# The first image's statistics ahead of the weights, and two input places in the second pass, in a two-layer convolution kernel

## The chip, the cores and the metric

The kernel runs on one core of a Trainium2 chip. The metric is the device time of one execution in microseconds (us). The engines are PE (TensorE), DVE (VectorE), ACT (ScalarE), POOL (GpSimd) and SP (SyncE), whose queue issues all of the kernel's transfers.

## The reference

The input x is 4 images of 64 channels and 256 x 256 pixels, in float32. Two layers follow each other, each with a residual.

```python
x = x + L0(_gn(x), ...)      # group norm, 32 groups
x = x + L1(_gn(x), ...)

# layer 0
h = gelu(conv3x3(x, c1_w) + c1_b)
xa, k = split(c1x1(h, c2_w, c2_b))                 # 64 channels each
xs = gelu(depthwise 3x1 (depthwise 1x3 (xa)))
mask = top 2 of 3 of softmax(mean(xs) @ gate_w.T)
out = xs + sum over 3 experts of mask * w3(w2(k) * w1(xs))     # ranks 2, 4, 8
return c1x1(out, proj_w, proj_b)

# layer 1
h = relu(batchnorm(conv3x3(x, quantized w1) + b1))
h = batchnorm(conv3x3(h, quantized w2) + b2)
return relu(h + x)
```

Quantizing needs the greatest absolute value of all weights of w1 and of w2: `round(w / scale)` with `scale = max|w| / 127`. The batch norms take their mean and variance over all four images, so each is a point at which everything before must be done.

## The kernel before

**Data.** An image lies in memory as 128 partitions (64 channels twice, for two rows) by 128 row pairs. A chunk is 8 row pairs (1 MB), 16 chunks an image, 64 in all. x, the result of layer 0 (t1), the input of layer 1 (y), and the two convolution results of layer 1 (h1, h2) go through DRAM in chunks.

**Head.** `weights()` (from L201) comes first. It loads three packed arrays, `mset` (960 KB: w1, w2, and two factors), `m64` (129 KB) and `m128` (612 KB), and makes from them everything that later steps need: `av`, `sh_bias`, `tap_bias`, `ends`, `outer`; by four small matmuls (L238, L247, L250, L253), which share one PSUM place, `wk`, `k_bias`, `pw3` and `pb3`; and the quantized `wq` for w1 and w2. For the last, DVE takes the maximum of each partition (L263), POOL takes the maximum over the partitions with `partition_all_reduce` (L265), and DVE scales, rounds and copies (L267 to L278). After that the 16 chunks of image 0 are loaded and DVE takes their statistics (L403); the first two working chunks of x are loaded (L481); POOL makes the first row sums and differences `front_v` (L501); `stats_end` turns the statistics into the normalized convolution weights `c1s` and `u12` and its bias.

**Loop.** Everything then goes by a written plan: `at(step, order, call, ...)` puts a call into a step at a place in it, and the plan is run in the order of its keys with each engine's instructions kept in that order. A step is 8 rows of one image in layer 0 (`F_STEPS` = 32 steps an image). In it PE runs the products of the first convolution (`front_conv_a`, `front_conv_b`), the taps (`front_taps_a`, `front_taps_b`) and the projection (all by `quarter`, L458); DVE does `front_butterfly` (L568, L569), the taps' horizontal part and the next image's statistics; POOL does `front_pad` (L488), `front_v` (L501) and `divide` (L451), a one-column memset called `tick`, which waits for PE and for which PE's next products wait. Layer 1's first pass (`conv1_*`) follows image by image.

**Second pass.** With `ss1` known, `conv2_load` (L1089) brings chunk i+3 of h1, ACT normalizes it (`conv2_affine`, L1094), ACT and DVE split it into two parts (`conv2_split`, L360 and L362), POOL adds neighbouring pixels (`conv2_add`, L367), and PE convolves (L316). The result goes to h2, except for the last `KEEP` chunks, which stay on chip.

**Places.** Inputs lie in a pool `ring` of three places and a pool `spare` of one. Layer 0 and layer 1's first pass take the spare place in every fifth or fourth chunk; the second pass loads into the ring alone and keeps one h2 chunk in the spare place.

**End.** For each chunk, with the kept ones first, y is loaded (L1203), ACT makes v = y * gn + shift (L1215), DVE makes h = h * ss2 + v (L1216) and max(h, 0) + y (L1217), and SP writes the output (L1219) and reads an h2 chunk (L1224) into a place that came free.

Of the kernel before, what the change touches and what calls it, by code (L numbers as in the profile page):

```python
# [9 lines left out]
F32 = mybir.dt.float32  # L10
# [44 lines left out]
NLOW = sum(LOWS)  # L55
GN_EPS = 1e-5
BN_EPS = 1e-5
KEEP = 14
QMAX = 127.0
ROUND = 12582912.0  # L60

# [2 lines left out]
def conv_preact_kernel(ctx: ExitStack, tc: tile.TileContext, io, col128, colset, col64):  # L64
# [4 lines left out]

    const = ctx.enter_context(tc.tile_pool(name="const", bufs=1))  # L70
    stat = ctx.enter_context(tc.tile_pool(name="stat", bufs=2))
    ring = ctx.enter_context(tc.tile_pool(name="ring", bufs=3))
    spare = ctx.enter_context(tc.tile_pool(name="spare", bufs=1))
    psum = ctx.enter_context(tc.tile_pool(name="psum", bufs=1, space=PSUM))
    dram = ctx.enter_context(tc.tile_pool(name="dram", bufs=1, space=DRAM))
# [20 lines left out]
    def flat(t):  # L96
        return t.rearrange("p a b -> p (a b)")

    RING = max(CPAIR * PW, (CPAIR + 1) * W)

    def place_in(name, fourth=False):
        return (spare if fourth else ring).tile([P, RING], F32, tag="in", name=name)

    def chunk_in(name, fourth):

        t = place_in(name, fourth)
        return t[:, 0 : CPAIR * PW].rearrange("p (a b) -> p a b", b=PW)

    def dense_in(name, n, fourth=False):

        return place_in(name, fourth)[:, 0 : n * W].rearrange("p (a b) -> p a b", b=W)

    layers = ExitStack()

# [58 lines left out]
    nc.vector.memset(eps, GN_EPS)  # L173
    eps_bn = const.tile([P, 1], F32, name="eps_bn")
    nc.vector.memset(eps_bn, BN_EPS)
    ones = const.tile([P, P], F32, name="ones")
    nc.vector.memset(ones, 1.0)
    zeros = const.tile([P, PW], F32, name="zeros")
    nc.vector.memset(zeros, 0.0)
# [18 lines left out]
    w_scale = {n: column(f"scale_{n}") for n in ("w1", "w2")}  # L198
    sh = c128("sh")

    def weights():  # L201

        mset = flat(chunk_x("mset"))[:, 0 : io["mset"].shape[1]]
        m64_t = work.tile([P, 2, GF], F32, tag="xs", name="m64", bufs=4)
        m64 = flat(m64_t)[0:C, 0 : io["m64"].shape[1]]
        nc.sync.dma_start(mset, io["mset"])
        nc.sync.dma_start(m64, io["m64"])
        nc.sync.dma_start(m128, io["m128"])

# [14 lines left out]
        nc.vector.tensor_scalar(tap_bias, sv_sum, sh_bias, c128("sv_b"), ALU.mult, ALU.add)  # L224
        for i in range(2):
            nc.vector.tensor_scalar(end[:, i : i + 1], sh[:, 2 * i : 2 * i + 1], c128("c2_ba"), None, ALU.mult)
        nc.vector.tensor_scalar(ends, end, sv_sum, None, ALU.mult)
        for i in range(2):
            o = outer[:, i, :]
            nc.vector.tensor_scalar(o, zeros[:, 0:W], sh_bias, None, ALU.add)  # L230
            nc.vector.tensor_tensor(o[:, 0 : W : W - 1], o[:, 0 : W : W - 1], end, ALU.subtract)
            nc.vector.tensor_scalar(o, o, c128("sv")[:, 2 * i : 2 * i + 1], None, ALU.mult)

        nc.vector.memset(wk, 0.0)
        ps = small("ps_wk")
        nc.tensor.matmul(ps[:, 0:NLOW], c64("c2_k"), c64("w2_t")[:, 0:NLOW], start=True, stop=True)  # L238

        for s in range(2):  # L240
            half = slice(s * C, s * C + C)
            for i in range(2):
                o = 16 * (i ^ s)
                nc.vector.tensor_copy(wk[half, s, i, o : o + NLOW], ps[half, 0:NLOW])
        nc.vector.memset(both, 0.0)
        ps = small("ps_kb")
        nc.tensor.matmul(ps[:, 0:1], c64("w2_t"), c64("c2_bk"), start=True, stop=True)  # L247
        nc.vector.tensor_tensor(k_bias, ps[:, 0:1], c128("e_b2"), ALU.add)
        ps = small("ps_pw3")
        nc.tensor.matmul(ps[:, 0:C], c64("w3"), c64("proj_t")[:, 0:C], start=True, stop=True)  # L250
        nc.vector.tensor_copy(pw3, ps[:, 0:C])
        ps = small("ps_pb3")
        nc.tensor.matmul(ps[:, 0:3], c64("proj_t"), c64("b3"), start=True, stop=True)  # L253
        nc.vector.tensor_copy(pb3, ps[:, 0:3])

        for name in ("w1", "w2"):  # L260
            w = cset(name)
            top = stat.tile([P, 1], F32, tag="s1", name=f"top_{name}")
            nc.vector.tensor_reduce(top, w, AX.X, ALU.max, apply_absolute_value=True)  # L263
            top_all = stat.tile([P, 1], F32, tag="s2", name=f"top_all_{name}")
            nc.gpsimd.partition_all_reduce(top_all, top, P, bass_isa.ReduceOp.max)  # L265
            scale = w_scale[name]
            nc.vector.tensor_scalar(scale, top_all, 1.0 / QMAX, None, ALU.mult)  # L267
# [201 lines left out]
    def front_alloc(b, k):  # L469
        c = b * NCH + k  # L470
        if c % 5 == 3:
            xs_of[b, k] = chunk_x(f"x_{b}_{k}")
        else:
            xs_of[b, k] = chunk_in(f"x_{b}_{k}", c % 5 == 4)

    def front_load(b, k):

# [328 lines left out]
    y_in, h_out, st_h = {}, {}, {}  # L806

    def conv1_load(b, k):
        y = y_in[b, k] = dense_in(f"yn_{b}_{k}", CPAIR + 1, k % 4 == 0)
        a = 1 if k == 0 else 0  # L810
        at_y = y[:, a:, :]
        nc.sync.dma_start(at_y, y_d[b][:, k * CPAIR + a - 1 : (k + 1) * CPAIR, :])
# [76 lines left out]
        nc.vector.bn_aggr(bn1[:, b, :], flat(st_h.pop(b)))  # L889


    weights()
    STATS_IN = (("s", 4),) * 4 + (("o", 3),) * 3
    for k in range(NCH):
        stats_load(0, k, *STATS_IN[k % 7])
# [2 lines left out]
    for k in range(2):  # L898
        front_alloc(0, k)
        front_load(0, k)  # L900

    first_v = ((0, 0), (0, 1), (1, 0))
    for n, half in first_v:
# [8 lines left out]
    for n, half in first_v:  # L912
        front_v(0, n, half, ((0, 3),))

    def at_each(places, chain):

        for place in places:
            at(*place, next, chain, None)

    F_STEPS = NOCT  # L920
    CONV1 = B * F_STEPS
# [185 lines left out]
        del h_in[i]  # L1107
        split_sums(sums2[i % 2], sums_in.pop(i))

    for i in range(3):  # L1110
        conv2_load(i)
    ss1 = const.tile([P, 2], F32, name="ss1")
    bn_affine(bn1, "g1", "be1", ss1, "bn1")
# [9 lines left out]

    def chunk_h2(b, k):
        n = next(h2_place) % KEEP
        if n == KEEP - 1:
            h2[b, k] = dense_in(f"h2_{b}_{k}", CPAIR, True)
        else:
            h2[b, k] = kept.tile([P, CPAIR, W], F32, tag="h2", name=f"h2_{b}_{k}", bufs=KEEP - 1)
        return h2[b, k]  # L1130

    def conv2(d):
# [23 lines left out]
    with tc.manual_schedule(  # L1156
        engines={
            mybir.EngineType.PE,
            mybir.EngineType.SP,
            mybir.EngineType.DVE,  # L1160
            mybir.EngineType.Pool,
            mybir.EngineType.Activation,
        }
    ):
        for cut in CUTS:
            conv2_affine(0, *cut)
            conv2_split(0, (cut,))
        conv2_add(0)
        conv2_sums(0)
        conv2_affine(1)  # L1170
        conv2_add(1)
        for d in range(2 * len(chunks)):
            i = d // 2
            opened = conv2(d)
            if d % 2 == 0:
                if i + 3 < len(chunks):
                    conv2_load(i + 3)
                if i + 1 < len(chunks):
                    conv2_split(i + 1)
                    conv2_sums(i + 1)  # L1180
            elif i + 2 < len(chunks):
                conv2_affine(i + 2)
                conv2_add(i + 2)
            conv2_out(d, *opened)


# [4 lines left out]

    halves_stack.close()
    end = ctx.enter_context(tc.tile_pool(name="end", bufs=2, reuse_waits="tile"))
    MORE = 6
    AHEAD = 3 + MORE - 1

    def end_load(i):
        b, k = steps[i]
        if i % (3 + MORE) < 3:
# [10 lines left out]
    for i, (b, k) in enumerate(steps):  # L1210
        if i + AHEAD < len(steps):
            end_load(i + AHEAD)
        y, h = y_of.pop(i), h2.pop((b, k))
        v = end.tile([P, CPAIR, W], F32, tag="v", name=f"v_{b}_{k}")
        nc.scalar.activation(v, y, AF.Identity, bias=shift[:, b : b + 1], scale=gn2[b][:, 1:2])  # L1215
        nc.vector.scalar_tensor_tensor(h, h, ss2[:, 0:1], v, ALU.mult, ALU.add)  # L1216
        nc.vector.scalar_tensor_tensor(h, h, 0.0, y, ALU.max, ALU.add)  # L1217
        for par in range(2):
            nc.sync.dma_start(out_v[b, par][:, k * CPAIR : (k + 1) * CPAIR, :], h[par * C : (par + 1) * C])  # L1219
# [117 lines left out]
```

## Time and profile before

| | |
|---|---|
| time, median of 3 runs | 3260.03 us (3255.96 to 3262.79) |
| time of the profiled execution | 3257.65 us |
| its span, first to last instruction | 3255.8 us |
| PE busy | 2664.0 us (82%) |
| DVE busy | 2665.1 us (82%) |
| ACT busy | 1647.6 us (51%) |
| POOL busy | 1603.1 us (49%) |
| moved by DMA | 832.01 MB, 256 GB/s in the mean |
| mean granted clock of TensorE | 0.924 |

How to read it: a row of a time line gives the start in us, the busy time in us, the engine, the line, the operation, what it writes and reads, how many instructions are merged in it, and in brackets the engine's idle time before it with what ended that. "SPq" and "POOLq" are queues: issuing and configuring, not counted as busy. "PEld" is TensorE's weight load. A digit of a slice row is the busy share of a fortieth of the span (81.4 us) in tenths.

### The profile page before, as it was taken

How to read it: one execution, taken by the hardware profiler on the slowest of the kernel's cores; microseconds unless marked ns; L12 is line 12 of the kernel's file. 1: busy time of each engine (PE TensorE's matmuls, PEld its weight loads, DVE VectorE, ACT ScalarE, POOL GpSimd, SP SyncE). 2: the span in 40 equal slices, each digit the busy share in tenths (PEclk: the TensorE clock that was granted, in tenths of full speed). 3: DMA queues.
4: the chain of work that ended last, by engine and by line, in shares of the span. 5: the costliest groups of instructions: out<-in, count | busy, mean ns of one | idle time of the engine just before them, and what ended most of it. 6: DMA issues, size and time to landing. Idle time of an engine off the chain costs nothing.

```text
span 3255.8 us, 61027 instructions
## 1 busy us (share of the span) xinstructions
PE 2664.0 (82%) x25080; PEld 1756.5 (54%) x25080; DVE 2665.1 (82%) x2810; ACT 1647.6 (51%) x1799; POOL 1603.1 (49%) x1833
## 2 busy tenths in 40 slices
PE   2999999999999999999999999989999999300000
PEld 1555555555555555555676677768787878200000
DVE  7676588878888777777899999979999999876655
ACT  0444443444434344446666666767777777432222
POOL 2444544444444534445687787757777777100000
PEclk9999999999999999999999999999999999655555
DMA  8665689879987777766788886656666663799999
GB/s 306 175 182 131 161 270 287 246 212 289 277 272 219 217 203 210 214 195 207 283 288 298 292 315 220 245 194 229 238 234 233 245 223 124 261 412 412 413 412 377
DMA packets 355591, 832.01 MB, mean 256 GB/s; under 512 B 22192, under 2 KB 284848, under 8 KB 293360
## 3 DMA queue, kind: packets, MB, share of 16 engines
q1 hardware_dynamic: 355312, 828.11, 76.5%
q8 instruction: 197, 3.23, 0.4%
q14 instruction: 82, 0.67, 0.1%
HBM read 489.85 MB, written 338.17 MB: 254 GB/s over the span
## 4 chain that ended last, share of the span: by engine, by line
PE 40%; SPq 10%; DVE 8%; DMA 3%; issue 3%; ACT 2%; POOL 1%; ACTq 0%; DVEq 0%; POOLq 0%
PE ps_h L316 22%; SPq L1224 7%; PE ps_c L458 5%; PE ps_h2m L316 4%; PE ps_a L458 3%; SPq L1219 2%; PE ps_hm L316 2%; DVE half L362 2%; DMA yn<-y_d 2%; DVE h L342 2%; PE ps_o L778 1%; PE ps_p L458 1%; SPq L1203 1%; DVE st_h L874 1%; DMA y_end<-y_d 1%
## 5 line engine op out<-in xcount | busy, mean ns | idle before, releaser
L316 PE MATMUL ps_h<-half,w_q 128*128 128x512 f32 x4096 | 1026.4, 402 | 20.4 <-DVE h L342 13.7
L316 PEld LDWEIGHTS ps_h<-half,w_q 128*128 128x128 f32 x4096 | 772.7, 190 | 249.4 <-DVE h L342 24.0
L381 POOL TENSOR_TENSOR sum<-s,sum 128x640 fp32r<-128x640 f32 (+1 forms) x256 | 557.2, 2197 | 199.4 <-ACT sum L379 193.8
L501 POOL TENSOR_TENSOR v_ring<-x 128x256 f32<-128x256 f32 x1024 | 591.2, 613 | 48.4 <-DMA x<-in_x 46.5
L458 PE MATMUL ps_c<-v_ring,u 64*64 64x256 f32 (+1 forms) x6472 | 389.1, 369 | 4.7 <-DVE u L429 3.5
L458 PE MATMUL ps_a<-h,av 64*64 64x512 f32 (+1 forms) x3568 | 383.5, 533 | 11.0 <-DVE t L628 8.6
L458 PE MATMUL ps_c<-v_ring,c1s 64*64 64x256 f32 (+1 forms) x6472 | 386.6, 370 | 5.0 <-POOL tick L451 4.5
L342 DVE SCALAR_TENSOR_TENSOR h<-ps_h,scale_w,m 128x1024 f32<-128x1024 f32 x256 | 326.7, 1276 | 73.0 <-ACT m L341 72.9
L575 ACT ACTIVATE h<-ps_c,c1b 128x512 f32<-128x512 f32 x256 | 174.1, 742 | 403.5 <-PE ps_c L458 403.5
L458 PEld LDWEIGHTS ps_c<-v_ring,c1s 64*64 64x64 f32 x6472 | 250.5, 133 | 202.3 <-issue 72.2
L458 PEld LDWEIGHTS ps_c<-v_ring,u 64*64 64x64 f32 x6472 | 270.4, 133 | 144.0 <-POOL v_ring L501 66.0
L451 POOL MEMSET tick<- 128x1 f32 x132 | 13.0, 98 | 679.2 <-PE ps_a L458 668.5
L645 ACT ACTIVATE xs<-t 128x1024 f32<-128x1024 f32 x128 | 135.4, 1058 | 368.9 <-DVE t L631 351.4
L1215 ACT ACTIVATE v<-y_end,shift,gn 128x2048 f32<-128x2048 f32 x64 | 133.8, 2092 | 293.8 <-DMA y_end<-y_d 260.9
L362 DVE TENSOR_TENSOR half<-h,half 128x1280 fp32r<-128x1280 f32 (+1 forms) x128 | 254.3, 2028 | 7.7 <-ACT half L360 7.7
L1216 DVE SCALAR_TENSOR_TENSOR h<-h,ss,v 128x2048 f32<-128x2048 f32 x64 | 149.9, 2349 | 134.5 <-ACT v L1215 84.4
L690 DVE TENSOR_TENSOR x<-ps_p,x 128x1024 f32<-128x1024 f32 x128 | 156.1, 1219 | 101.1 <-PE ps_p L458 69.0
L568 DVE TENSOR_TENSOR ps_c<-m,ps_c 128x512 f32<-128x512 f32 x128 | 89.0, 695 | 175.8 <-ACT m L567 175.7
L458 PEld LDWEIGHTS ps_a<-h,av 64*64 64x64 f32 x3568 | 163.5, 133 | 128.5 <-issue 91.7
L362 DVE TENSOR_TENSOR half<-yn,half 128x1280 fp32r<-128x1280 f32 x80 | 202.7, 2551 | 0.0
L341 ACT ACTIVATE m<-ps_hm,m,scale_w 128x512 f32<-128x512 f32 x128 | 99.4, 777 | 183.2 <-PE ps_hm L316 153.9
L786 DVE SCALAR_TENSOR_TENSOR y<-ps_o,ob,y 128x1024 f32<-128x1024 f32 x128 | 163.6, 1278 | 15.1 <-PE ps_o L778 10.9
(186 smaller groups left out, 4083.5 us busy)
## 6 DMA issues: line engine op xcount, KB each, us to landing
h_d<-h SPq DMA_DIRECT2D x114, 1024.0 KB, 4.8
h<-h_d SPq DMA_DIRECT2D x64, 1152.0 KB, 7.1
yn<-y_d SPq DMA_DIRECT2D x60, 1152.0 KB, 8.3
xs_in<-in_x SPq DMA_DIRECT2D x64, 1024.0 KB, 9.0
x<-in_x SPq DMA_DIRECT2D x256, 256.0 KB, 5.3
y<-t_d SPq DMA_DIRECT2D x64, 1024.0 KB, 8.8
y_d<-y SPq DMA_DIRECT2D x256, 256.0 KB, 5.1
y_end<-y_d SPq DMA_DIRECT2D x64, 1024.0 KB, 10.8
```

The costliest lines, as they stand in the source:

```text
L316: nc.tensor.matmul(ps[:, 0 : n * HW], w[:, k, m, :], t[:, i + m : i + m + n, c : c + HW], start=(j == 0), stop=(j == len(terms) - 1),)
L342: nc.vector.scalar_tensor_tensor(h.rearrange("p a (b e) -> p e (a b)", e=2), by_two(ps)[:, :, 0 : n * HW], w_scale[w], m.unsqueeze(1).to_b ...
L362: engine.tensor_tensor(lower, y, upper.bitcast(F32), ALU.subtract)
L381: nc.gpsimd.tensor_tensor(tiles[1][:, a:e, :], t, tiles[0][:, a:e, :].bitcast(F32), ALU.subtract)
L458: last[:] = [nc.tensor.matmul(ps[o, at_out[0] : at_out[1], :], w[i], rhs[i], **flags)]
L501: nc.gpsimd.tensor_tensor(v_of(p)[:, o : o + 2, :], *terms[p])
L575: nc.scalar.activation(h.rearrange("p q (c e) -> p e q c", e=2), c[:, t].rearrange("p (e q c) -> p e q c", e=2, q=GP), AF.Gelu, bias=c1_bi ...
L645: nc.scalar.activation(flat(xss[b, n]), flat(open_t.pop((b, n))), AF.Gelu, accum_out=pooled[b][:, n : n + 1])
L690: nc.vector.tensor_tensor(t1, ps, t1, ALU.add)
L786: nc.vector.scalar_tensor_tensor(y, ps.rearrange("p i a b -> p (i a) b"), out_bias[b], y, ALU.add, ALU.add)
L1216: nc.vector.scalar_tensor_tensor(h, h, ss2[:, 0:1], v, ALU.mult, ALU.add)
L1224: nc.sync.dma_start(chunk_h2(b2, k2), h2_d[b2][:, k2 * CPAIR : (k2 + 1) * CPAIR, :])
```

## The change

It has four parts.

1. `weights()` becomes a generator in six pieces. Only the load of `m128` and two memsets stay ahead of image 0's statistics. The loads of `mset` and `m64` come after the loads of x's first two chunks. The four other pieces are put into the loop: `av` to `outer` at (0, 8.2), the small matmuls at (1, 8.2), w1's quantizing at (1, 12), w2's at (2, 8.2).
2. `ring` has two places and `spare` two, with tags of their own. In the loops that use all four (or five, with `chunk_x`) the order of the places is the same. The second pass loads its third chunk after the first one has been split, and chunk i+3 in the odd half of chunk i, when chunk i+1 has been split.
3. `KEEP` is 15: one h2 chunk more stays on chip, in the second spare place.
4. At the end ACT scales h in place, and DVE adds y; v and its two places are gone, and y has nine places as before (two and seven). `ones` moves to another pool.

```diff
-KEEP = 14
+KEEP = 15
-    ring = ctx.enter_context(tc.tile_pool(name="ring", bufs=3))
+    ring = ctx.enter_context(tc.tile_pool(name="ring", bufs=2))
...
-    def place_in(name, fourth=False):
-        return (spare if fourth else ring).tile([P, RING], F32, tag="in", name=name)
+    def place_in(name, apart=None):
+        if apart is None:
+            return ring.tile([P, RING], F32, tag="in", name=name)
+        return spare.tile([P, RING], F32, tag=f"in{apart}", name=name)
...
-    ones = const.tile([P, P], F32, name="ones")
+    ones = lconst.tile([P, P], F32, name="ones")
...
-    def weights():
+    def weights(end=end):
         mset = flat(chunk_x("mset"))[:, 0 : io["mset"].shape[1]]
...
+        nc.sync.dma_start(m128, io["m128"])
+        nc.vector.memset(wk, 0.0)
+        nc.vector.memset(both, 0.0)
+        yield
         nc.sync.dma_start(mset, io["mset"])
         nc.sync.dma_start(m64, io["m64"])
-        nc.sync.dma_start(m128, io["m128"])
+        yield
...
-        nc.vector.memset(wk, 0.0)
+        yield
         ps = small("ps_wk")
...
-        nc.vector.memset(both, 0.0)
...
         for name in ("w1", "w2"):
+            yield
             w = cset(name)
...
-            xs_of[b, k] = chunk_in(f"x_{b}_{k}", c % 5 == 4)
+            xs_of[b, k] = chunk_in(f"x_{b}_{k}", {2: 0, 4: 1}.get(c % 5))
...
-        y = y_in[b, k] = dense_in(f"yn_{b}_{k}", CPAIR + 1, k % 4 == 0)
+        y = y_in[b, k] = dense_in(f"yn_{b}_{k}", CPAIR + 1, {3: 0, 0: 1}.get(k % 4))
...
-    weights()
+    parts = weights()
+    next(parts)
     STATS_IN = (("s", 4),) * 4 + (("o", 3),) * 3
...
     for k in range(2):
         front_alloc(0, k)
         front_load(0, k)
+    next(parts)
...
+    at_each(((0, 8.2), (1, 8.2), (1, 12), (2, 8.2)), parts)
...
-    for i in range(3):
+    for i in range(2):
         conv2_load(i)
...
-        if n == KEEP - 1:
-            h2[b, k] = dense_in(f"h2_{b}_{k}", CPAIR, True)
+        if n >= KEEP - 2:
+            h2[b, k] = dense_in(f"h2_{b}_{k}", CPAIR, n - (KEEP - 2))
...
         conv2_sums(0)
+        conv2_load(2)
         conv2_affine(1)
...
             if d % 2 == 0:
-                if i + 3 < len(chunks):
-                    conv2_load(i + 3)
                 if i + 1 < len(chunks):
                     conv2_split(i + 1)
                     conv2_sums(i + 1)
-            elif i + 2 < len(chunks):
-                conv2_affine(i + 2)
-                conv2_add(i + 2)
+            else:
+                if i + 3 < len(chunks):
+                    conv2_load(i + 3)
+                if i + 2 < len(chunks):
+                    conv2_affine(i + 2)
+                    conv2_add(i + 2)
             conv2_out(d, *opened)
...
-    MORE = 6
-    AHEAD = 3 + MORE - 1
+    MORE = 7
+    AHEAD = 2 + MORE - 1
...
-        v = end.tile([P, CPAIR, W], F32, tag="v", name=f"v_{b}_{k}")
-        nc.scalar.activation(v, y, AF.Identity, bias=shift[:, b : b + 1], scale=gn2[b][:, 1:2])
-        nc.vector.scalar_tensor_tensor(h, h, ss2[:, 0:1], v, ALU.mult, ALU.add)
+        nc.scalar.activation(h, h, AF.Identity, bias=shift[:, b : b + 1], scale=ss2[:, 0:1])
+        nc.vector.scalar_tensor_tensor(h, y, gn2[b][:, 1:2], h, ALU.mult, ALU.add)
         nc.vector.scalar_tensor_tensor(h, h, 0.0, y, ALU.max, ALU.add)
```

More of the change, by code (lines that the diff above doesn't have):

```diff
@@ L99, in conv_preact_kernel, with chunk_in, dense_in @@
     RING = max(CPAIR * PW, (CPAIR + 1) * W)
-    def place_in(name, fourth=False):
-        return (spare if fourth else ring).tile([P, RING], F32, tag="in", name=name)
-    def chunk_in(name, fourth):
-        t = place_in(name, fourth)
+    def place_in(name, apart=None):
+        if apart is None:
+            return ring.tile([P, RING], F32, tag="in", name=name)
+        return spare.tile([P, RING], F32, tag=f"in{apart}", name=name)
+    def chunk_in(name, apart):
+        t = place_in(name, apart)
         return t[:, 0 : CPAIR * PW].rearrange("p (a b) -> p a b", b=PW)
-    def dense_in(name, n, fourth=False):
-        return place_in(name, fourth)[:, 0 : n * W].rearrange("p (a b) -> p a b", b=W)
+    def dense_in(name, n, apart=None):
+        return place_in(name, apart)[:, 0 : n * W].rearrange("p (a b) -> p a b", b=W)
     layers = ExitStack()
@@ L913, in conv_preact_kernel, with at_each @@
         front_v(0, n, half, ((0, 3),))
-    def at_each(places, chain):
+    def at_each(places, pieces):
         for place in places:
-            at(*place, next, chain, None)
+            at(*place, next, pieces, None)
+    at_each(((0, 8.2), (1, 8.2), (1, 12), (2, 8.2)), parts)
     F_STEPS = NOCT
@@ L1125, in chunk_h2 @@
         n = next(h2_place) % KEEP
-        if n == KEEP - 1:
-            h2[b, k] = dense_in(f"h2_{b}_{k}", CPAIR, True)
+        if n >= KEEP - 2:
+            h2[b, k] = dense_in(f"h2_{b}_{k}", CPAIR, n - (KEEP - 2))
         else:
-            h2[b, k] = kept.tile([P, CPAIR, W], F32, tag="h2", name=f"h2_{b}_{k}", bufs=KEEP - 1)
+            h2[b, k] = kept.tile([P, CPAIR, W], F32, tag="h2", name=f"h2_{b}_{k}", bufs=KEEP - 2)
         return h2[b, k]
@@ L1193, in conv_preact_kernel @@
     end = ctx.enter_context(tc.tile_pool(name="end", bufs=2, reuse_waits="tile"))
-    MORE = 6
-    AHEAD = 3 + MORE - 1
+    MORE = 7
+    AHEAD = 2 + MORE - 1
     def end_load(i):
         b, k = steps[i]
-        if i % (3 + MORE) < 3:
+        if i % (2 + MORE) < 2:
             y_of[i] = dense_in(f"y_end_{b}_{k}", CPAIR)
```

## The prediction

> **What bounds the kernel now.** I read the page first, then the head of the time line, because the change moves the head's work. The busy table says that PE carries the span; the slices say where it does not.
>
> ```profile
> PE 2664.0 (82%) x25080; PEld 1756.5 (54%) x25080; DVE 2665.1 (82%) x2810; ACT 1647.6 (51%) x1799; POOL 1603.1 (49%) x1833
> PE   2999999999999999999999999989999999300000
> DMA  8665689879987777766788886656666663799999
> ```
>
> PE is full from the second slice to the end of layer 1's second pass. Whatever delays PE early is therefore not made up later. Before 66 us PE waits for the first image's statistics, and after 2805 us transfers set the pace.
>
> In the time line of the head (start, us, engine, line) three rows hold PE: the reduction over partitions, the statistics, and the first products.
>
> ```profile
> 7.46 0.95 DVE L263 TENSOR_REDUCE top_w<-mset 128x1 f32<-128x768 f32 x1
> 9.86 0.72 POOL L265 PARTITION_ALL_REDUCE top_all_w<-top_w  x2 [9.40 <-issue]
> 10.26 0.15 DVE L267 TENSOR_SCALAR scale_w<-top_all_w 128x1 f32<-128x1 f32 x1 [1.85 <-POOL top_all_w L265]
> ...
> 20.64 36.26 DVE L403 BATCH_NORM_STATS2 st_x<-xs_in 128x6 f32<-128x512 f32 x61
> ...
> 57.10 3.47 POOL L501 TENSOR_TENSOR v_ring<-x 128x256 f32<-128x256 f32 x6 [46.53 <-DMA x<-in_x]
> ...
> 66.24 3.29 PE L458 MATMUL ps_c<-v_ring,u 64*64 64x256 f32 x32 [3.46 <-DVE u L429]
> ```
>
> DVE does weights until 20.6, then 61 statistics without a gap (0.594 each). The same time line puts the first w1 maximum (L263) at 5.86 to 6.81, yet POOL reduces it at 9.86 with "issue" as its reason. The source views of L265 and L501 show what lies there: POOL's configuration is changed before the reduction and again before the next elementwise work.
>
> ```profile
> L265 POOLq MODIFY_POOL_CONFIG  x2: 11/11/11, 1.0 to 1.0; - x2
> L501 POOLq MODIFY_POOL_CONFIG  x2: 83/83/83, 10.5 to 10.6; - x2
> ```
>
> From the first change (1.04) to the first reduction is 8.8 us. This switch is the price that decides here.
>
> **The change, part by part.** Times marked "after" are worked out on the old time line.
>
> *Statistics first.* 960 KB and 129 KB (1.115 MB) leave the queue ahead of the image; at the 419 GB/s of the window 20 to 40 that is 2.7 us. The last statistics load was issued at 40.33 and landed 11.5 later, at 51.8; after, 49.1. DVE no longer starts late, so it ends one chunk behind the landing, 49.1 + 4 x 0.594 = 51.5 instead of 56.9: 5.4 us earlier. The image's first working chunk (fourth piece issued at 42.7, landing 14.2 later) comes at 54.3, POOL's six first products take 3.5, ending 57.8, about when the group statistics (62.98) arrive at 57.6. So POOL holds nothing up and PE starts at 60.8 instead of 66.24: **-5.4**.
>
> *Step 0.* Fourteen DVE instructions (av to outer, by the head's rows 3.3 us) go behind the first butterfly, which ends at 73.0 - 5.4 = 67.6. With the three statistics (1.87) they end at 72.8; the next butterfly could start at 78.25 - 5.4 = 72.85. Hidden. If mset landed later than 67.6 they would show; it is queued behind x's second chunk, which landed at 62.8: 62.8 - 2.7 + 0.98 MB / 412 GB/s = 62.5.
>
> *Step 1.* Four small matmuls stand on PE behind the products that ended at 77.23, now 71.8. All use one PSUM place, so each waits for DVE to empty the one before, and the first emptying stands on DVE behind the butterfly that ends at 74.4. Then: wk copies 0.5, matmul 0.6, k_bias 0.2, matmul 0.7, copy 0.25, matmul 0.6, with about 0.05 between: PE goes on at 77.5 instead of 72.4. **+5.1**; what waits behind them on PE is all of step 2. So the gain of the head is spent here. pb and the w1 maximum then end at 78.6.
>
> *The reductions, steps 1 and 2.* In the order of the changed program POOL has, from step 1 on: eight products, change of configuration, reduction of w1, tick of step 2, change, four products, change, reduction of w2, change, four products, pad, tick of step 3. Four switches stand in the queue that feeds PE, where before both lay ahead of 57 us. PE waits for each tick (L451) and for the products (L501). With 8.8 us a switch:
>
> - step 1's products end at 75.17 + 4.61 - 5.4 = 74.4; switch, 83.2; reduction 0.4, 83.6; tick 83.7 (before 81.84);
> - switch, 92.5; four products (2.3), 94.8; switch, 103.6; reduction, 104.0; the w2 maximum is there at about 91.5;
> - switch, 112.8; products 115.1; pad 0.33; tick of step 3 at 115.4.
>
> The ticks of steps 2 and 3 in the time line of before:
>
> ```profile
> 81.84 0.10 POOL L451 MEMSET tick<- 128x1 f32 x1 [2.06 <-PE ps_c L458]
> 90.33 0.10 POOL L451 MEMSET tick<- 128x1 f32 x1 [3.51 <-PE ps_a L458]
> ```
>
> That is **+25.1** at step 3, with the -5.4 and +5.1 already in it. PE has run out of work at about 100.6. After that step the old pattern repeats, so the delay stays.
>
> The price is seen once only, for the way to the reduction, beside a full DMA. Its bounds: 8.8 from the change to the first use, or 3.05 if only what came after the input (6.81 to 9.86) counts; the way back is not exposed and could be anything from 0 to 46 us. I take 8.8 for all four, because the way back shows no surcharge at first use: x landed at 56.9 and POOL began at 57.10. So the work is done from the change on, and the excess alone is not the price. With 3.05 each, the reductions come at 81.7 and 93.1 and the tick of step 3 at 99.2: +8.9. With 0, DVE's w1 work, the butterfly, the w2 maximum and the rewrite of mset (whose place x's fourth chunk takes) put it at 91.9: +1.6.
>
> The Trainium skill (GPSIMD Engine Reference, Instruction dispatch) states that the first call of a freshly loaded kernel pays an instruction load of about 6 us, without an instruction in the profile that shows it. The trace has 8.8 in all and 3.05 beyond the wait. By the page the tick would come at 104.8, an estimate of +14.5, and the whole at about 3271.
>
> PE is idle for about 15 us before step 3. After its first idle time the 32 products took 3.29 us, in the next steps 1.96: **+1.3**.
>
> *Two places in the second pass.* The load of chunk i+3 now waits until DVE has split chunk i+1, not i. One chunk of the time line:
>
> ```profile
> 2514.21 0.37 SPq L1089 DMA_DIRECT2D h<-h_d  x1
> 2515.00 3.99 DVE L362 TENSOR_TENSOR half<-h,half 128x1280 fp32r<-128x1280 f32 x2
> 2526.38 2.31 ACT L1094 ACTIVATE h<-h,ss 128x2304 f32<-128x2304 f32 x1
> ```
>
> The load moves from 2514.2 to 2519.1. The store ahead of it (2513.78, 4.8 us) is then through, and loads that run alone land in 5.0 us (2690 to 2770): 2524.1, while ACT asks for it at 2526.38. Even with the 7.1 us of now it comes at 2526.2. On SP the next store (2523.14) is queued behind it and loses nothing. **0**; without that cover each us late would cost 60 us. The third load (2161.86) moves to 2190.1 and is asked for at 2197.4: 0.
>
> *The end.* One chunk less goes out and comes back. The store lies beside a full PE: 0. The read lies in the stage that transfers bound. In the windows (busy PE, PEld, DVE, ACT, POOL, then clock, DMA share, GB/s) DMA is full to the end, and empty just before the first output:
>
> ```profile
> 2905.00:3200.00 295.00, 0.00 (x0) 0.00 (x0) 179.32 (x78) 81.58 (x39) 0.00 (x0) 0.50 1.04 412
> 2808.00:2813.00 5.00, 0.00 (x0) 0.00 (x0) 5.00 (x3) 4.39 (x3) 0.00 (x0) 0.50 0.00 0
> ```
>
> 1.05 MB at 412 GB/s is **-2.5**. One y load that ran early at 2764 now runs after the second pass; it fits into the 5 us in which nothing moves. DVE keeps two instructions of the same shape a chunk. ACT scales h instead of y: 2.09 us either way, ahead of DVE. Giving up v's places costs nothing, as nine y loads still run ahead.
>
> **Sum.** 25.1 + 1.3 - 2.5 = +23.9 on the profiled execution's 3257.65 (span 3255.8): 3281.6, given as 3282. The median of the runs is 3260.03, 2.4 above that execution. A measurement of this kernel can tell about 0.2% (6.5 us) from no change.
>
> **Rivals.**
>
> - *The switches cost nothing in the loop* (POOL loads early, or both codes stay). Then +1.6 - 2.5: 3256.7, no change. For it: no row shows the way back. Against: 8.8 us at the start with the input there. It decides when a switch is below about 2.5 us. 0.10.
> - *Only the excess counts* (3.05 each): 8.9 + 1.3 - 2.5: 3265.4, slower by a little. Against it: the first products after the way back were not late. 0.20; a part of it falls within 0.2% of the median.
> - *Faster:* switches free, and PE makes up step 1's stall in the short waits of steps 2 and 3 (0.66 and 0.63 us in the rows at 84.61 and 97.68, too little for 5.1): 3257.65 - 5.4 - 2.5 = 3249.8. 0.03.
> - *Dearer:* the way back takes half as much again as the way there, 4.4 more twice: 3290. 0.12.
>
> The forecast itself has 0.55. Low end 3264, at the excess alone; high end 3291, at the dearer way back. Slower 0.85, same 0.12, faster 0.03.
>
> **What would show it.** Statistics ending near 51.5; PE starting near 61; four configuration changes, with POOL idle after each for 8 to 9 us; the tick of step 3 near 115; the same step length after it; second pass unchanged; last stage shorter by 2.5. The forecast is wrong if POOL's products follow a configuration change within 3 us, if the tick of step 3 comes before 97, or if ACT waits for h loads in the second pass.

## The result and the profile after

| | before | after |
|---|---|---|
| time, median of 6 runs each | 3259.14 us (3255.96 to 3262.79) | 3274.66 us (3270.64 to 3278.05) |
| time of the profiled execution | 3257.65 us | 3273.53 us |
| its span | 3255.8 us | 3271.7 us |
| first product of PE | 66.24 us | 58.50 us |
| tick of step 3 / step 5 | 90.33 / 110.6 us | 108.69 / 130.8 us |
| last batch-norm aggregation | 2798.1 us | 2818.4 us |
| from there to the end | 457.7 us | 453.3 us |

The changed kernel is slower: the ratio of its time to that of before is 1.0048, 95% interval 1.0035 to 1.0061. In the spans that is 15.9 us.

Line numbers of the changed kernel differ from those of before: the reduction over partitions is L273 (L265), the row sums of POOL are L509 (L501), the tick is L459 (L451), the products are L466 (L458), the statistics are L411 (L403).

The busy table and the slice row of PE, from the page of the kernel after:

```profile
PE 2672.1 (82%) x25080; PEld 1761.4 (54%) x25080; DVE 2665.2 (81%) x2810; ACT 1646.4 (50%) x1799; POOL 1604.7 (49%) x1833
PE   2799999999999999999999999989999999400000
```

The number of instructions is the same on every engine. Only PE's busy time grew by more than 2 us, by 8.1, and the second digit of its slices fell from 9 to 7. So the loss lies in the first 160 us, and with PE full behind it nothing makes up for it.

The head, from the time line of the kernel after (start, busy us, engine, line, operation, and the idle time ahead of it in brackets):

```profile
46.37 2.47 DVE L411 BATCH_NORM_STATS2 st_x<-xs_in 128x6 f32<-128x512 f32 x4 [1.65 <-DMA xs_in<-in_x]
...
51.27 3.46 POOL L509 TENSOR_TENSOR v_ring<-x 128x256 f32<-128x256 f32 x6 [50.82 <-DMA x<-in_x]
...
58.50 3.69 PE L466 MATMUL ps_c<-v_ring,u 64*64 64x256 f32 x32 [3.45 <-DVE u L437]
```

Statistics, POOL's first products and PE all begin earlier than before. That part of the change does what it says: 7.7 us. What follows on POOL takes more than all of it away. POOL's time line of the kernel after, from step 1 to the tick of step 3:

```profile
67.95 4.76 POOL L509 TENSOR_TENSOR v_ring<-x 128x256 f32<-128x256 f32 x8
80.48 0.38 POOL L273 PARTITION_ALL_REDUCE top_all_w<-top_w  x1 [7.78 <-issue]
83.37 0.10 POOL L459 MEMSET tick<- 128x1 f32 x1 [2.50 <-PE ps_c L466]
90.67 2.32 POOL L509 TENSOR_TENSOR v_ring<-x 128x256 f32<-128x256 f32 x4 [7.21 <-issue]
98.78 0.38 POOL L273 PARTITION_ALL_REDUCE top_all_w<-top_w  x1 [5.79 <-issue]
106.08 2.32 POOL L509 TENSOR_TENSOR v_ring<-x 128x256 f32<-128x256 f32 x4 [6.92 <-issue]
...
108.69 0.09 POOL L459 MEMSET tick<- 128x1 f32 x1
```

Four times POOL sits idle with "issue" as the reason, that is, with nothing that the profile shows to wait for: 7.78, 7.21, 5.79 and 6.92 us, together 27.7. The source views of the two lines name what lies there: a change of POOL's configuration ahead of each.

```profile
L273 POOLq MODIFY_POOL_CONFIG  x4: 1/2/4, 72.7 to 93.2; - x4
L509 POOLq MODIFY_POOL_CONFIG  x6: 11/11/83, 1.0 to 99.2; - x6
```

The changes come in pairs of rows. Those of the loop stand at 72.7, 83.5, 93.2 and 99.1, each just behind POOL's last work, and each idle time runs from there to the first use.

On PE, in its time line of the kernel after, the small matmuls and the waits for POOL:

```profile
69.93 0.39 PE L246 MATMUL ps_wk<-m 64*128 64x14 f32 x2
74.21 0.55 PE L254 MATMUL ps_kb<-m 64*128 64x1 f32 x2 [3.89 <-DVE wk L252]
...
76.53 3.69 PE L466 MATMUL ps_c<-v_ring,u 64*64 64x256 f32 x32
...
91.33 3.69 PE L466 MATMUL ps_c<-v_ring,u 64*64 64x256 f32 x32 [5.85 <-POOL v_ring L509]
...
108.83 1.98 PE L466 MATMUL ps_c<-v_ring,c1s 64*64 64x256 f32 x20 [9.68 <-POOL tick L459]
```

PE comes back from the small matmuls 6.6 us after their start (69.93 to 76.53) and then waits for POOL's products and for the tick. After each of these gaps 32 products take up to 3.69 us; undisturbed, as in the kernel before, they take 1.96:

```profile
77.85 1.96 PE L458 MATMUL ps_c<-v_ring,u 64*64 64x256 f32 x32 [0.62 <-issue]
```

The granted clock of TensorE shows the difference: 0.50 in the kernel after from 76.5 to 80.0, from 91.3 to 95.0 and from 108.8 to 112.0, and 1.00 in the kernel before from 77.9 to 81.7. This is called half clock below.

### The profile page after: what moved, and what is told of

It is laid out like the page before. It is cut to its first block, busy times and chain, and to the rows that moved or that the text cites. A ratio compares the mean times of both kernels' runs of the same rounds, so it can differ in the third digit from the quotient of the medians.

```text
span 3271.7 us, 60952 instructions
## 1 busy us (share of the span) xinstructions
PE 2672.1 (82%) x25080; PEld 1761.4 (54%) x25080; DVE 2665.2 (81%) x2810; ACT 1646.4 (50%) x1799; POOL 1604.7 (49%) x1833
## 4 chain that ended last, share of the span: by engine, by line
PE 65%; DVE 12%; SPq 10%; DMA 5%; issue 3%; ACT 3%; POOL 1%; DVEq 0%; POOLq 0%; ACTq 0%
PE ps_h L324 24%; PE ps_c L466 17%; PE ps_a L466 9%; SPq L1237 4%; PE ps_h2m L324 3%; SPq L1217 3%; PE ps_o L786 3%; PE ps_p L466 3%; PE ps_hm L324 2%; SPq L1232 2%; PE ps_k L663 2%; PE ps_q L712 2%; DVE half L370 2%; DMA yn<-y_d 1%; DVE h L350 1%
## 5 line engine op out<-in xcount | busy, mean ns | idle before, releaser
L509 POOL TENSOR_TENSOR v_ring<-x 128x256 f32<-128x256 f32 x1024 | 591.6, 613 | 66.3 <-DMA x<-in_x 50.8
L466 PE MATMUL ps_c<-v_ring,u 64*64 64x256 f32 (+1 forms) x6472 | 393.8, 373 | 9.3 <-POOL v_ring L509 5.9
L466 PE MATMUL ps_c<-v_ring,c1s 64*64 64x256 f32 (+1 forms) x6472 | 389.3, 372 | 14.6 <-POOL tick L459 14.0
L466 PE MATMUL ps_a<-h,av 64*64 64x512 f32 (+1 forms) x3568 | 384.7, 535 | 11.0 <-DVE t L636 8.5
L583 ACT ACTIVATE h<-ps_c,c1b 128x512 f32<-128x512 f32 x256 | 174.7, 745 | 429.9 <-PE ps_c L466 429.9
L466 PEld LDWEIGHTS ps_c<-v_ring,c1s 64*64 64x64 f32 x6472 | 252.3, 134 | 212.4 <-issue 74.5
L466 PEld LDWEIGHTS ps_c<-v_ring,u 64*64 64x64 f32 x6472 | 272.2, 134 | 150.6 <-POOL v_ring L509 70.6
L459 POOL MEMSET tick<- 128x1 f32 x132 | 12.9, 98 | 678.3 <-PE ps_a L466 673.4
L1228 ACT ACTIVATE h<-h,shift,ss 128x2048 f32<-128x2048 f32 x64 | 132.4, 2089 | 274.1 <-DMA h<-h_d 272.7
L1229 DVE SCALAR_TENSOR_TENSOR h<-y_end,gn,h 128x2048 f32<-128x2048 f32 x64 | 149.9, 2351 | 129.3 <-DMA y_end<-y_d 123.8
L698 DVE TENSOR_TENSOR x<-ps_p,x 128x1024 f32<-128x1024 f32 x128 | 156.2, 1220 | 100.5 <-PE ps_p L466 75.0
L466 PEld LDWEIGHTS ps_a<-h,av 64*64 64x64 f32 x3568 | 164.0, 133 | 128.9 <-issue 92.2
```

Of the source, the lines that this page charges most:

```text
L466: last[:] = [nc.tensor.matmul(ps[o, at_out[0] : at_out[1], :], w[i], rhs[i], **flags)]
L509: nc.gpsimd.tensor_tensor(v_of(p)[:, o : o + 2, :], *terms[p])
L583: nc.scalar.activation(h.rearrange("p q (c e) -> p e q c", e=2), c[:, t].rearrange("p (e q c) -> p e q c", e=2, q=GP), AF.Gelu, bias=c1_bi ...
L698: nc.vector.tensor_tensor(t1, ps, t1, ALU.add)
L1228: nc.scalar.activation(h, h, AF.Identity, bias=shift[:, b : b + 1], scale=ss2[:, 0:1])
L1229: nc.vector.scalar_tensor_tensor(h, y, gn2[b][:, 1:2], h, ALU.mult, ALU.add)
```

## The experiments

Step n is the nth turn of the loop, counted from 0, and its tick is the POOL memset at its middle, for which PE waits. The ticks of before: step 2 at 81.8, 3 at 90.3, 4 at 99.8, 5 at 110.6; of after: 83.4, 108.7, 120.0, 130.8. Ratios are to the kernel before. Theory: the four configuration changes in the queue that feeds PE make the loss. Rivals: the small matmuls' stall, or the rest of the change (second pass, end).

### The two halves of the change

**e1: the head of before, all else changed.**

```diff
-    parts = weights()
-    next(parts)
+    weights()
...
-    next(parts)
...
-    at_each(((0, 8.2), (1, 8.2), (1, 12), (2, 8.2)), parts)
```

with `weights()` as it was before.

> The changed kernel with the head of before: weights first, then the statistics; the two input places, 15 kept chunks and the end stay changed. Theory A (the whole loss lies in the head, +20.3 us at the fifth tick; the end gains 4.4): about 3254.7 against 3259.1. Its rival here (the end gains only the read of one chunk, 2.5, and the rest of the 4.4 is chance): about 3256.6. If the two places cost anything in the second pass, more than 3259; the stage from the first normalizing of the second pass to the last statistics should take 614.9 us as before.

Measured: 3254.93 us, ratio 0.9985 [0.9975, 0.9994]. The ticks stand where they stood before (91.0 and 111.2), and the last stage (from the last batch-norm aggregation to the end) is 454.0 us.

**e2: only the new head,** in the kernel before (the opposite edit).

> The kernel before with the new head alone; three ring places, 14 kept chunks and the old end. If the parts add: 3259.1 + 20.3 = 3279.4, with the tick of step 3 at 108.7 and that of step 5 at 130.8. If the places matter for the head (the mset place, the ring): another time for the ticks.

Measured: 3278.42 us, ratio 1.0062 [1.0047, 1.0077]. Ticks of steps 3 and 5 at 108.4 and 130.9, last stage 458.2.

So the two halves add up: -0.0015 and +0.0062 make +0.0047, and the whole change has +0.0048. All of the loss is in the head, and the rest of the change is a small gain.

### The switches of POOL

**e3: both maxima side by side, so two switches and not four.**

```diff
         for name in ("w1", "w2"):
-            yield
...
+            nc.vector.tensor_reduce(top, cset(name), AX.X, ALU.max, apply_absolute_value=True)
...
+            nc.gpsimd.partition_all_reduce(top_all[name], top, P, bass_isa.ReduceOp.max)
+        for name in ("w1", "w2"):
+            if name == "w2":
+                yield
...
-            nc.gpsimd.partition_all_reduce(top_all, top, P, bass_isa.ReduceOp.max)
```

> The changed kernel with both reductions over partitions side by side in step 1, so that POOL changes its configuration twice in the loop instead of four times; same arithmetic. Theory A (each change holds up POOL by some 7 us, and PE waits for POOL): PE then waits for its own taps, the tick of step 3 comes at about 99.3 instead of 108.7, and the time falls by 10 to about 3264.5. Rival B (PE's waits for the four small matmuls and its half clock make the loss, the changes lie beside them): tick of step 3 within 2 us of 108.7, about 3274.

Measured: 3262.84 us, ratio 1.0012 [1.0003, 1.0021]. POOL's time line of this kernel:

```profile
80.20 0.72 POOL L273 PARTITION_ALL_REDUCE top_all_w<-top_w  x2 [7.18 <-issue]
83.59 0.10 POOL L463 MEMSET tick<- 128x1 f32 x1 [2.68 <-PE ps_c L470]
90.46 5.08 POOL L513 TENSOR_TENSOR v_ring<-x 128x256 f32<-128x256 f32 x8 [6.77 <-issue]
...
99.63 0.10 POOL L463 MEMSET tick<- 128x1 f32 x1 [3.76 <-PE ps_a L470]
```

The second reduction follows the first without an idle time, so the price is one of changing and not one of reducing. Two switches fewer bring the tick of step 3 from 108.7 to 99.6, and the whole from 1.0048 to 1.0012.

**e4: no switch.** The maximum over partitions is found without POOL: DVE multiplies each partition's maximum into a matrix of ones, PE turns that with a unit matrix (packed behind the weights), and DVE takes the maximum along the row.

```diff
+            nc.vector.tensor_scalar(spread[:, i * P : i * P + P], ones, top, None, ALU.mult)
...
+            nc.tensor.matmul(ps[:, at_i], spread[:, at_i], cset("eye"), start=True, stop=True)
...
+        nc.vector.tensor_reduce(tops, ps.rearrange("p (a b) -> p a b", b=P), AX.X, ALU.max)
...
-            nc.gpsimd.partition_all_reduce(top_all, top, P, bass_isa.ReduceOp.max)
...
-    at_each(((0, 8.2), (1, 8.2), (1, 12), (2, 8.2)), parts)
+    at_each(((0, 8.2), (1, 8.2), (1, 12), (2, 4), (2, 8.2)), parts)
```

> The changed kernel with the maximum over partitions taken by two matmuls with the unit matrix (which is loaded as part of mset) and a DVE reduction, so that POOL never changes its configuration in the loop; the small matmuls still wait for each other. Theory A: the tick of step 3 at about 91.7 (before: 90.3), the time about 3256. Rival B: tick of step 3 at 100 or later and 3268 or more, since the stall of the small matmuls (6 us) and the half clock stay.

Both maxima are now taken at (1, 12), the two products stand at (2, 4), and w1 and w2 are quantized together at (2, 8.2); w1 was quantized in step 1 before.

Measured: 3256.52 us, ratio 0.9992 [0.9983, 1.0002]. The source view of POOL's row sums has changes of configuration only at the kernel's start:

```profile
L518 POOLq MODIFY_POOL_CONFIG  x2: 11/11/11, 0.8 to 0.8; - x2
```

Most of the loss is gone: the tick of step 5 is at 116.6, not 130.8. It is still 6.0 later than before, though the loop begins earlier (tick of step 0 at 62.1, before 69.6). POOL's time line says why:

```profile
93.86 0.33 POOL L505 TENSOR_SCALAR x<-zeros,gn 128x16 f32<-128x16 f32 x1 [7.30 <-DVE w_q L295]
94.12 0.10 POOL L468 MEMSET tick<- 128x1 f32 x1
```

The pad of x's fourth chunk waits for DVE, since that chunk takes the place of `mset`, which DVE is still quantizing. Part of this wait is the experiment's own, since w1's quantizing now stands ahead of w2's in the same step.

### The small matmuls

**e5: the four small matmuls in one PSUM place,** one after the other, the switches kept.

```diff
-        ps = small("ps_wk")
+        ps = small("ps_w")
...
-        ps = small("ps_kb")
-        nc.tensor.matmul(ps[:, 0:1], c64("w2_t"), c64("c2_bk"), start=True, stop=True)
...
+        nc.tensor.matmul(ps[:, 16:17], c64("w2_t"), c64("c2_bk"), start=True, stop=True)
```

and the other two likewise, at columns 32 and 128; all copies follow.

> The changed kernel with its four changes of POOL's configuration, but the four small matmuls of step 1 write different columns of one PSUM place, so that PE need not wait between them. Theory A (POOL's changes are the path, PE's stall of 6.6 us lies mostly beside the first of them): POOL reduces at about 80.4 as before, the tick of step 2 comes at 81 instead of 83.4, that of step 3 at about 106.3, and the time falls by some 2.4 to 3272. Rival (the stall of 5 to 6.6 us counts in full): tick of step 3 at 102 to 103.5, about 3268.

Measured: 3271.38 us, ratio 1.0037 [1.0022, 1.0051]. PE's time line of this kernel has the stall gone, but a wait in its place:

```profile
71.80 1.96 PE L458 MATMUL ps_c<-v_ring,u 64*64 64x256 f32 x32
...
82.04 1.98 PE L458 MATMUL ps_c<-v_ring,c1s 64*64 64x256 f32 x16 [6.06 <-POOL tick L451]
```

PE goes on at 71.8 instead of 76.5, and then waits 6.06 us for the tick, since POOL is still in its first switch. The tick of step 3 moves by 1.0 us only, from 108.7 to 107.7: POOL's tick of step 2 no longer waits 2.5 us for PE, but in this execution its first change came 0.9 us later (73.6 against 72.7). While the switches are there, the stall lies mostly beside them. POOL's time line has the four again, and DVE's the input of the first:

```profile
74.67 0.94 DVE L263 TENSOR_REDUCE top_w<-mset 128x1 f32<-128x768 f32 x1
...
81.57 0.38 POOL L265 PARTITION_ALL_REDUCE top_all_w<-top_w  x1 [7.96 <-issue]
...
89.16 2.32 POOL L501 TENSOR_TENSOR v_ring<-x 128x256 f32<-128x256 f32 x4 [7.17 <-issue]
97.35 0.38 POOL L265 PARTITION_ALL_REDUCE top_all_w<-top_w  x1 [5.86 <-issue]
105.06 2.32 POOL L501 TENSOR_TENSOR v_ring<-x 128x256 f32<-128x256 f32 x4 [7.33 <-issue]
```

The first reduction comes 6.0 us after its input (75.6).

### Where the gain of the head could be kept

**e6: e4, and `mset` in a spare place,** that of x's fifth chunk.

```diff
-        mset = flat(chunk_x("mset"))[:, 0 : io["mset"].shape[1]]
+        mset = place_in("mset", 1)[:, 0 : io["mset"].shape[1]]
```

> e4 (no change of configuration in the loop) with mset in the spare place of x's fifth chunk instead of the place of the fourth, so that the pad of the fourth chunk on POOL need not wait for the quantizing of w2. If that wait (7.3 us idle on POOL, 3.8 on PE at the tick of step 3) is what is left of e4: tick of step 3 at about 90.6 instead of 94.1, step 3 about 9.5 long instead of 11.7, and the time 5 less, about 3251. If something else holds the tick: still about 94 and 3256.

Measured: 3257.06 us, ratio 0.9997 [0.9988, 1.0006]. The tick of step 3 came about as expected (91.7), and step 3 then took 14.4 us (before: 9.5), so the gain was lost again. From the time line:

```profile
91.73 6.08 POOL L518 TENSOR_TENSOR v_ring<-x 128x256 f32<-128x256 f32 x8
...
95.27 0.83 DVE L293 TENSOR_TENSOR w_q<-mset 128x256 fp32r<-128x256 f32 x1
...
100.51 1.88 PE L475 MATMUL ps_c<-v_ring,c1s 64*64 64x256 f32 x20 [4.00 <-DVE ps_c L586]
```

The wait has changed its engine. Quantizing w1 and w2 is one block on DVE, ahead of the butterfly for which PE waits 4.00 us. It is also slow there: the same L293 took 0.42 us where POOL was idle.

**e7: e6 and the one PSUM place of e5.**

> All three together: no change of configuration, mset in the fifth chunk's place, the small matmuls in one PSUM place. PE starts at 58.4 as in the changed kernel, 7.8 before the old start, and should lose only the small matmuls (about 1.5) and the two products for the maxima (0.7): tick of step 3 at about 84.7 (before 90.3). With the changed end (3.7 less in the last stage, mean of the changed kernel, e1, e3 and e4 against before and e2): 3258.7 - 5.6 - 3.7 = about 3249.4, faster than both kernels. If step 1 or 2 has another wait behind these: 3253 or more.

Measured: 3251.35 us, ratio 0.9975 [0.9966, 0.9984]. Tick of step 3 at 86.5, of step 4 at 102.1: step 3 took 15.6 us, behind the same block. The time is not explained by the head, whose tick of step 5 (112.9) is later than before. The last stage has 3.7 of the 9.0 us by which its span is shorter. Another 5.7 lie in the stretch from the first to the second batch-norm aggregation of the first pass, which lasted 172.5 to 178.8 us in the profiled executions here, 178.8 in that of before, and 174.7 in that of e8, whose code there is that of before. What sets it was not settled; as before and e8 differ by 4.1 us there, most of the 5.7 can be chance.

**e9: e7, with w1 quantized in step 2 and w2 in step 3.**

```diff
         for i, name in enumerate(("w1", "w2")):
+            if i:
+                yield
...
-    at_each(((0, 8.2), (1, 8.2), (1, 12), (2, 4), (2, 8.2)), parts)
+    at_each(((0, 8.2), (1, 8.2), (1, 12), (2, 4), (2, 8.2), (3, 8.2)), parts)
```

> As e7 (no configuration switch, one PSUM place for the small matmuls), and w1 is quantized in step 2, w2 in step 3 instead of both in step 2. If the 7 to 8 us block of quantizing on VectorE in front of the third butterfly made step 3 of e7 last 15.6 us instead of 9.4 to 9.9, each half (about 3.7 us) hides better: tick of step 4 at 96 to 98 instead of 102.1, the later ticks 4 to 6 us earlier, the whole about 3246. If the length of step 3 comes from something else (the half clock, or TensorE's order), the tick of step 4 stays at 102 and the whole at 3251.

Measured: 3252.6 us, ratio 0.9978 [0.9969, 0.9987]. Mostly a miss: the tick of step 4 is at 100.5. In step 3 PE waits for another DVE result, the taps' horizontal part, which now stands behind w2:

```profile
97.20 3.16 PE L469 MATMUL ps_a<-h,av 64*64 64x512 f32 x20 [4.14 <-DVE t L639]
```

**e11: e9, with w2 behind the taps of step 3.**

```diff
-    at_each(((0, 8.2), (1, 8.2), (1, 12), (2, 4), (2, 8.2), (3, 8.2)), parts)
+    at_each(((0, 8.2), (1, 8.2), (1, 12), (2, 4), (2, 8.2), (3, 12.5)), parts)
```

> As e9, but w2 is quantized in step 3 behind the taps' horizontal part, not in front of it. In e9 TensorE was idle for 4.14 us in step 3, waiting for that part. If VectorE's 3.9 us in front of the taps are the cause, the idle time goes, step 3 lasts 10 to 11 us instead of 14.2, the tick of step 4 comes at 96 to 97.5 instead of 100.5, that of step 5 at 106 to 108 instead of 111.5 (before: 110.6), and the whole is 4 us below e9, about 3248.5. If something else makes step 3 long, the ticks stay at 100.5 and 111.5. Between step 5 and the last statistics the profiled executions of all kernels so far lasted 2682 to 2691 us, so the ticks decide, not the whole.

Measured: 3246.77 us, ratio 0.9957 [0.9943, 0.9971]. The tick of step 4 came at 95.3, 0.7 us ahead of the range expected, and that of step 5 at 106.4, within it. The same row in this kernel's time line:

```profile
93.18 1.95 PE L469 MATMUL ps_a<-h,av 64*64 64x512 f32 x20 [0.63 <-DVE t L639]
```

The idle time of 4.14 is 0.63, and 20 products take 1.95 us and not 3.16 (granted clock 1.00 from 93.2 to 95.1, in e9 0.60 from 97.2 to 100.3). This version beats both kernels. Of the 12.9 us between the medians (3259.70 for before in the same series), the tick of step 5, 4.2 us earlier than before, and the kept chunk (2.5, below) explain some 7; the stretch of the first pass named at e7 has 4.6 in the profiled execution (174.2 us), and what sets that stays open.

**e12: w1 behind the taps of step 3, w2 behind those of step 4** (places (3, 12.5) and (4, 12.5)).

> As e11, but w1 is quantized behind the taps of step 3 and w2 behind those of step 4. Step 2 loses its 3.4 us of quantizing; if they hid there in e9 (the butterfly behind them waited for ScalarE), the tick of step 3 stays at 86.4, step 4 takes what step 3 took in e11, and the tick of step 5 is not earlier than in e11. If they cost something in step 2, the tick of step 3 comes at 84.7 to 85.5.

Measured: 3247.14 us, ratio 0.9963 [0.9951, 0.9976], the same time as e11 within the intervals. The tick of step 3 stays (85.7, in e11 85.9), so w1 cost nothing in step 2; that of step 5 is 1.7 later than in e11 (108.1). POOL's time line shows the next place of the wait:

```profile
107.84 0.33 POOL L499 TENSOR_SCALAR x<-zeros,gn 128x16 f32<-128x16 f32 x1 [7.21 <-DVE w_q L289]
```

The pad of x's fifth chunk, which takes the place of `mset`, waits for the quantizing of w2, as in e4 that of the fourth. Moved further back, the block has left the butterfly and the taps and meets the place's next user.

### The end

**e8: before, with only the arithmetic of the end exchanged** (ACT scales h in place, DVE adds y).

```diff
-        nc.scalar.activation(v, y, AF.Identity, bias=shift[:, b : b + 1], scale=gn2[b][:, 1:2])
-        nc.vector.scalar_tensor_tensor(h, h, ss2[:, 0:1], v, ALU.mult, ALU.add)
+        nc.scalar.activation(h, h, AF.Identity, bias=shift[:, b : b + 1], scale=ss2[:, 0:1])
+        nc.vector.scalar_tensor_tensor(h, y, gn2[b][:, 1:2], h, ALU.mult, ALU.add)
```

> The kernel before, in which only the last stage's arithmetic is changed: ACT scales h in place, DVE adds y; 14 kept chunks, three ring places. The last stage (from the aggregation of the second pass's last statistics to the end) takes 457.7 and 458.2 with the old end, 453.3 to 455.2 with the new. If the gain beyond the read of one chunk (2.5) comes from ACT running ahead on h: about 456.6. If the swap is worth nothing: 457.7 to 458.2. If the swap is most of it: 455 or less.

Measured: 3258.27 us, ratio 0.9997 [0.9987, 1.0007], last stage 457.7 as before. The exchange is worth nothing.

**e10: e1 with 14 chunks kept** (`KEEP = 14`, one h2 chunk in the spare places).

> The rest of the change alone (two input places, exchanged arithmetic at the end, head of before), but 14 chunks kept as before. If the kept chunk's read is what shortens the last stage, the last stage is back at 457 to 458 us (454.0 with 15 kept) and the whole at about 3258; if the read is worth nothing and the end gains by the order of the loads, it stays at 454 and 3255.

Measured: 3258.66 us, ratio 0.9999 [0.9990, 1.0007], last stage 456.4. Without the kept chunk the gain of e1 is gone. One execution's last stage varies by more than the effect, so the means are the better reading: 457.5 over the four profiled executions with 14 chunks kept (457.7, 458.2, 457.7, 456.4), and 455.0 over the ten with 15 kept (453.3 to 457.7). That is 2.5 us for the chunk, though single executions of the two kinds overlap.

## Why the prediction came out as it did

The direction and the mechanism were right; the size was not: +23.9 us were forecast, +15.5 came in the medians and +15.9 in the spans. By its own steps:

- **Statistics first, -5.4: came as -7.7.** They ended at 48.8, not 51.5. The step reckoned only with the bytes that leave the queue. But the statistics' loads wait for places that DVE empties (SP waited 26.1 us for DVE's statistics before, 19.0 after), and DVE no longer began late: the last of them was issued at 29.5, 10.8 us earlier than the 40.3 from which the step started. DVE had it at 46.4, where the step had it land at 49.1:

```profile
29.50 0.33 SPq L404 DMA_DIRECT2D xs_in<-in_x  x1
```

- **Small matmuls, +5.1: came larger on PE,** 6.6 us from their start to the next products where the forecast had 5.7 (71.8 to 77.5), and half clock behind it (3.69 and 3.20 us for two blocks of 32 products). But most of it lies beside the first switch: what is left of it on POOL is the 2.5 us for which the tick of step 2 waited. e5 takes the stall out and gains 1.0 us at the tick of step 3.
- **The switches, 4 x 8.8: the term that was mis-sized.** They took 7.78, 7.21, 5.79 and 6.92 us, 27.7 in place of 35.2. The one switch seen in the kernel before (8.8) was dearer than each of these. That the way back costs as much as the way there, and that the price runs from the change on whether the input is there or not, was right: the first switch took 7.78 us with its input there 5.0 us after the change (77.66, from the row below), and in e5 7.96 with its input there after 2.0. Working the POOL queue through with the measured values: 72.7 (end of step 1's products, expected 74.4) + 27.7 + 0.8 for the reductions + 4.6 for the products + 0.4 for pad and tick + 2.5 of waiting for PE, which the forecast did not have, gives 108.7, and there the tick is (expected 115.4).

```profile
76.72 0.94 DVE L271 TENSOR_REDUCE top_w<-mset 128x1 f32<-128x768 f32 x1
```

- **The Trainium skill's rule** (GPSIMD Engine Reference, Instruction dispatch: about 6 us of code loading at the first call of a freshly loaded kernel) gave an estimate of 104.8 for that tick and 3271 for the whole. Measured were 108.7 and 3274.66, so this estimate came closer than the sum with the 8.8 of the kernel's start. But each of these four switches but one took over 6.9 us, and the rows put a change of configuration, which the profile shows, ahead of each.
- **Half clock, +1.3: came as 1.8,** the growth of the delay from the tick of step 3 (18.4) to that of step 4 (20.2). The granted clock behind the tick of step 3 was 0.50, and 20 products took 1.98 us where they took 1.09 before. PE had been idle for 9.68 us, where the forecast had some 15. That the sizes are near is partly luck: the row from which the 1.3 was read (66.24, 3.29 us) shows a granted clock of 1.00 (66.2 to 69.5), so why it was slow is not shown. Later the delay is 19.2 to 22.1 at the aggregations of the first pass and 20.3 at the last one.
- **Second pass, 0: right.** The load of a chunk moved towards its use, as the time line of the kernel after shows, and ACT took the same pace, one chunk in 9.4 us:

```profile
2539.36 0.32 SPq L1101 DMA_DIRECT2D h<-h_d  x1
...
2546.68 2.31 ACT L1106 ACTIVATE h<-h,ss 128x2304 f32<-128x2304 f32 x1
```

  It is now issued 7.3 us ahead of its use (before: 12.2), and the median landing time of these loads fell from 7.1 to 5.0 us. e1 has the part alone: from the last batch-norm aggregation of the first pass to that of the second it took 620.5 us as before.
- **The end, -2.5: right.** The kernel after shows -4.4 in its one execution, the means at e10 -2.5. e8 shows that the exchange gives nothing, and e10 that the rest without the 15th chunk gives no gain clear of the scatter (456.4); so the chunk is left as the source.

Of the rivals, "the switches cost nothing" falls to the idle times and to e3 and e4. "Only the excess counts" (3.05 each) falls to the three later switches, which took 5.79 to 7.21 us with their inputs there. The first one alone can't tell, since its reduction came 2.8 us after its input; in e5 it came 6.0 after, and so the rival falls there too. "Faster" falls to the measured time. "The way back is dearer" is refuted: 7.21 and 6.92 against 7.78 and 5.79.

The sum with the measured terms: 18.4 at the tick of step 3, 1.8 of half clock, -4.4 at the end: 15.8, against 15.9 in the spans.

## What to carry to other kernels

Before work is moved from an idle stretch into a full loop, look at what each of its instructions drags along on its queue: here two reductions of 0.38 us cost 27.7 us of POOL's time, because POOL's configuration is changed to them and back. Group such instructions, do them where nobody waits for POOL, or give the work to another engine. When a wait is taken away, look at the next instruction that stands behind the moved work: the gain of the head was paid to the POOL pad (e4, e12), to the butterfly (e6, e7) and to the taps (e9), and came through at the ticks only when the block stood behind the step's last result that PE waits for (e11, and all but 1.7 us of it in e12).

## What was not expected of the hardware

- Going back from the reduction to elementwise work costs as much as going to it (7.21 and 6.92 us), while the tick, a memset, ran between the two without a change (83.37, with the change behind it at 83.5). The second way there took 5.79, 5.84 and 5.86 us in the three kernels with four switches (after, e2, e5), the first one 7.78, 6.86 and 7.96; what makes the first dearer was not settled.
- DVE's quantizing and POOL's row sums slow each other down. In e6 and e7 the same DVE instructions took 0.42 us with POOL idle and 0.83 beside its row sums, a cast 0.29 and 0.70, and POOL's eight row sums 6.08 instead of 4.61. The Trainium skill (SBUF — State Buffer, SBUF: two separate sides) has a pair of ports that DVE and POOL share, and which the one that starts first locks for its whole instruction; that both lose time here agrees with it, but no run here separated that cause.
- The last stage, bound by transfers all through, varied by 4 us between kernels that are the same there (453.3 to 457.7 with 15 kept chunks), more than the effect that was looked for.
